# Layer 0's rows go back to node order through DRAM and indirect DMAs in a two-layer graph network kernel

## The chip, the cores and the metric

The kernel runs on one core of a Trainium2 chip. The metric is the time of one execution on the device, in microseconds. A core has a matrix engine (PE, with its weight loads listed apart as PEld), a vector engine (DVE), a scalar engine (ACT), GpSimd (POOL), and SyncE (SP), which here issues all DMAs. Each engine works through its own queue in order. TensorE's results go to PSUM, which PE writes and DVE and ACT read; POOL works on SBUF.

## The reference

There are 128 graphs of 128 nodes with 64 features, and a weighted adjacency matrix each. Layer 0 sums a two-layer edge function over the edges; layer 1 aggregates with the weights and applies a small network. Both have a residual and a layer norm. Cut to what is computed:

```
mask = adj > 0
h    = relu(x @ W1a [row j] + (x[j] - x[k]) @ W1b + b1)      # for every pair j, k
hm   = sum over k of h * mask
x    = layernorm(x + hm @ W2 + deg * b2)                     # layer 0
agg  = adj @ x
h    = elu(elu(agg @ V1 + c1) @ V2 + c2)
x    = layernorm(x + h @ V3 + c3)                            # layer 1
```

## The kernel before

Two graphs form a pair, and there are 64 pairs. The kernel uses that the masks are sparse. In a pair it counts each row's edges, ranks the rows by that count, and permutes them, so that rows with many edges stand together and are given many slots, and rows with few edges few. Edge sums are then dense matmuls with one-hot columns.

`prepare(p)` makes the mask `mk` on POOL (L419), the degrees on DVE, a key on POOL (`degb`, `keyc`, L427 and L428), and from it `pos`, for each row its place in sorted order (f32, 128 x 2, one column for each graph). `permb` (L450) is the permutation as a bf16 matrix. `sort_mask` (from L541) sorts the mask by two matmuls (L547), and by two more (L550) makes the inverse permutation. All four land in one PSUM bank; ACT copies the halves out as `mtp` (L555) and `permT` (L557, f32). `sort_x` and `project_a` sort and project the features; POOL splits the projections in bf16 parts `cp` (L493, L495) and computes `sa` and `corr`.

The units of the main loop are (pair, 3 feature groups, 3 banks): ACT seeds a PSUM bank `e` (L714), PE adds matmuls with the one-hot matrix (L725, L729), DVE reduces with absolute values into `sums` (L739).

`finish(p)` closes a pair. POOL subtracts the correction (`hm`, L642), PE projects to 64 outputs for each graph (L646 to L653), ACT copies the result to SBUF as `ys` (L657; 128 x 130, the two graphs' rows in sorted order and the degrees), and SP sends the degrees away (L659). `unsort` then brings the rows back to node order on PE: an identity matmul with `xx` puts the residual into the bank (L662) and a matmul with `permT` for each graph adds the rows (L664). `norm` copies the bank to `y` on ACT (L597), takes mean and variance on DVE (`st` L603, `ve` L605), the inverse root on POOL (`rs`, L610), the bias on DVE (`nb`, L613), and applies both on ACT (L619). The result `x1` is layer 0's output. Layer 1 follows: aggregation (L671), two hidden layers with `elu`, the last matmuls (L693 to L696), again `norm`, and the output DMA (L700). Each pair's loads (L406, L408) are issued three pairs ahead.

The order of the work is made by a planner, `Flow`, while the program is built. Every piece of work is a generator step that names its engine, an estimated cost, the events it needs and how many PSUM banks out of four. The planner always emits the step that can start first on its own clocks, with due times to break near ties. An event is the step's end by these clocks plus a lag of 0.2 us. A second name such as `PORT` makes steps on different engines exclude each other in the plan. Costs and events fix only the order in each queue; on the chip, semaphores make each instruction wait for its data. `ROUND` (13.0) is the planned length of a pair and `AHEAD` (3) how many pairs early preparation begins. A fallback for denser masks (`dense`) follows and isn't entered with this input.

Of the kernel before, what the change touches and what calls it, by code (L numbers as in the profile page):

```python
# [31 lines left out]
F32 = mybir.dt.float32  # L32
BF16 = mybir.dt.bfloat16
I32 = mybir.dt.int32
# [12 lines left out]
def gnn_kernel(ctx: ExitStack, tc: tile.TileContext, x, adj, w1, b1, w2, b2,  # L47
               v1, c1, v2, c2, v3, c3, out):
    nc = tc.nc
    B, N, F = x.shape  # L50
# [216 lines left out]
    with ExitStack() as fast:  # L267
        loads = fast.enter_context(tc.tile_pool(name="loads", bufs=8))
        prep = fast.enter_context(tc.tile_pool(name="prep", bufs=4))
        work = fast.enter_context(tc.tile_pool(name="work", bufs=4))  # L270
        ps_e = fast.enter_context(tc.tile_pool(name="ps_e", bufs=1, space=bass.MemoryType.PSUM))
        ps_m = fast.enter_context(tc.tile_pool(name="ps_m", bufs=1, space=bass.MemoryType.PSUM))
        sparse(tc, locals())
# [76 lines left out]
def sparse(tc, env):  # L350
# [5 lines left out]
    loads, prep, work, ps_m = g.loads, g.prep, g.work, g.ps_m  # L356
# [17 lines left out]
    PACE = ROUND / (3 * NB)  # L374
    STEP = 1.3
# [9 lines left out]
    def event(*key):  # L385
        return EV.setdefault(key, [])

    def happened(ev, *key):
        event(*key)[:] = ev
# [5 lines left out]
    def act(n, pointers=0):  # L395
        return 0.07 + 0.09 * pointers + n / 1200
# [4 lines left out]
    def pool(n):  # L401
        return 0.15 + n * 0.0022
# [7 lines left out]
    def flat(t):  # L410
        return t.rearrange("p s n -> p (s n)")

    def prepare(p):
# [38 lines left out]
        ev, = yield ("DVE PORT", 0.36, [ev], 0, permute)  # L452
# [88 lines left out]
    def sort_mask(p, ev):  # L541
# [3 lines left out]
        def sort(t):  # L545
            for s in range(2):
                nc.tensor.matmul(t[:, s * N:(s + 1) * N], d["mk"][:, s, :], permb[:, s, :],  # L547
                                 start=True, stop=True)
            for s in range(2):
                nc.tensor.matmul(t[:, (2 + s) * N:(3 + s) * N], permb[:, s, :], identb,  # L550
                                 start=True, stop=True)
        ev, t = yield ("PE", 0.33, [ev], 1, sort)
        mtp = d["mtp"] = prep.tile([P, 2, N], BF16, name="mtp", bufs=7)
        permT = d["permT"] = prep.tile([P, 2, N], F32, name="permT", bufs=7)
        evm, = yield ("ACT", act(2 * N), [ev], 0, lambda: nc.scalar.copy(flat(mtp), t[:, :2 * N]))  # L555
        happened(evm, "mtp", p)
        ev, = yield ("ACT", act(2 * N), [ev], 0, lambda: nc.scalar.copy(flat(permT), t[:, 2 * N:]))  # L557
        flow.give(t, ev)
        happened(ev, "permT", p)
# [34 lines left out]
    def norm(yps, ev, name):  # L594

        y = work.tile([P, 2, O], F32, name="y", bufs=6)
        evy, = yield ("ACT", act(2 * O), [ev], 0, lambda: nc.scalar.copy(flat(y), yps[:, :2 * O]))  # L597
# [3 lines left out]
        def stats():  # L601

            nc.vector.bn_stats(st.rearrange("p s t -> p (s t)"),  # L603
                               yps[:, :2 * F].rearrange("p (s f) -> p f s", s=2))
            nc.vector.tensor_scalar(ve, st[:, :, 2], 1.0 / F, EPS, op0=OP.mult, op1=OP.add)  # L605
        ev, = yield ("DVE", 0.38, [ev, evy], 0, stats)
        flow.give(yps, ev)
# [28 lines left out]
    def finish(p):  # L636
# [24 lines left out]
        def unsort(t):  # L661
            nc.tensor.matmul(t[:, :2 * O], ident, flat(xx), start=True, stop=False)  # L662
            for s in range(2):
                nc.tensor.matmul(t[:, s * O:(s + 1) * O], d["permT"][:, s, :],  # L664
                                 ys[:, s * O:(s + 1) * O], start=False, stop=(s == 1))
        ev, t = yield ("PE", 0.6, [ev, event("permT", p)], 1, unsort)
        x1, ev = yield from norm(t, ev, "x1")

# [30 lines left out]
        o, ev = yield from norm(t, ev, "o")  # L699
# [277 lines left out]
```

## Time and profile before

| | us |
|---|---|
| median of 3 runs | 928.74 |
| lowest and highest of them | 928.43, 929.03 |
| the profiled execution | 928.32 |
| its span in the trace | 925.7 |
| PE busy | 867.1 |
| DVE busy | 813.8 |
| ACT busy | 717.3 |
| POOL busy | 506.6 |

A profile comes from one execution. Its span runs from the first to the last instruction of the program, and 2.6 us lie around it. An engine's busy time is the time in which at least one of its instructions runs; shares are of the span or of a stretch of it. TensorE's granted clock was 0.991 of full speed in the mean. In the list of waits, a row names the engine and line that waited, what it waited for, the total us, how often, and the longest. In a tile's view the three numbers are shortest, median and longest duration in ns, then the first and the last start.

Three groups that the change touches look like this (busy us in all, mean ns of one):

| line and work | count | busy us | mean ns |
|---|---|---|---|
| L557, ACT copies `permT` | 64 | 24.3 | 380 |
| L597, ACT copies `y` (both layers) | 128 | 33.4 | 261 |
| L603, DVE statistics | 128 | 36.8 | 288 |

### The profile page before, as it was taken

Reading aid. Unit: us, or ns where it says so; the run is one execution under the profiler, and the core shown is the slowest. Engines: PE = TensorE matmul, PEld = TensorE weight load, DVE = VectorE, ACT = ScalarE, POOL = GpSimd, SP = SyncE. Lnnn points to the kernel's source line nnn. Section 1 sums busy time; section 2 is a strip of 40 time slices with the busy share of each in tenths; the row PEclk is TensorE's granted clock in tenths of the full one; section 3 lists DMA queues with packets and bytes.
Section 4 is the critical chain, followed back from the end, with each engine's and each line's share of the span. In section 5 each row is a group of like instructions: output and inputs, shape, how many; then the busy total and the mean of one; then the engine's idle time right before and its main releaser. Section 6 shows DMA issues by size and latency. Waiting matters only on the chain. (4 is left out here: it accounts for less than half of the span.)

```text
span 925.7 us, 19643 instructions
## 1 busy us (share of the span) xinstructions
PE 867.1 (94%) x6739; PEld 556.4 (60%) x6740; DVE 813.8 (88%) x2278; ACT 717.3 (77%) x2050; POOL 506.6 (55%) x654
## 2 busy tenths in 40 slices
PE   2689999999999999999999999999999999999994
PEld 1456666665665665666665666666666666666663
DVE  7699889989989989989989989999999999999972
ACT  0577887788788788788788788888878887888772
POOL 1565555665556565556565556565556555555521
PEclk9999999999999999999999999999999999999996
DMA  1100100100110110110100010110011001000000
GB/s 29 43 10 21 25 15 21 24 21 16 24 24 13 24 24 14 24 25 12 25 23 15 22 24 12 25 24 16 21 25 24 16 21 25 16 23 22 7 8 12
DMA packets 63580, 18.84 MB, mean 20 GB/s; under 512 B 46257, under 2 KB 63474, under 8 KB 63474
## 3 DMA queue, kind: packets, MB, share of 16 engines
q1 hardware_dynamic: 63474, 17.52, 8.1%
q8 instruction: 55, 0.90, 0.4%
q14 instruction: 51, 0.42, 0.1%
HBM read 13.24 MB, written 4.19 MB: 19 GB/s over the span
## 5 line engine op out<-in xcount | busy, mean ns | idle before, releaser
L739 DVE TENSOR_REDUCE sums<-e 128x56 f32<-128x504 f32 (+3 forms) x768 | 395.0, 542 | 33.6 <-PE e L725 16.9
L714 ACT COPY e<-aj 128x504 f32<-128x504 f32 (+2 forms) x768 | 366.1, 486 | 74.3 <-DVE sums L739 67.4
L725 PE MATMUL e<-oh,cp 128*128 128x504 bf16 (+1 forms) x1152 | 281.7, 375 | 1.8 <-ACT e L714 1.7
L610 POOL TENSOR_TENSOR rs<-ve,mhalf 128x2 f32<-128x2 f32 x128 | 90.6, 708 | 228.2 <-DVE ve L605 223.9
L725 PEld LDWEIGHTS <-cp 128*128 128x128 bf16 x1152 | 106.1, 97 | 89.5 <-DVE sums L739 1.1
L729 PE MATMUL e<-oh,cp 128*64 128x504 bf16 (+1 forms) x1152 | 157.5, 382 | 1.1 <-ACT e L714 1.1
L572 DVE TENSOR_TENSOR oh<-vp,slotc 128x1008 bf16<-128x1008 bf16 (+2 forms) x256 | 153.9, 601 | 3.2 <-ACT vp L564 3.0
L642 POOL TENSOR_TENSOR hm<-sums,corr 128x384 f32<-128x384 f32 x64 | 73.6, 1151 | 45.8 <-DVE sums L739 42.3
L629 ACT ACTIVATE e<-m,mone 128x256 f32<-128x256 f32 x128 | 62.6, 489 | 32.4 <-PE m L688 30.9
L493 POOL CAST cp<-r 128x512 bf16<-128x512 f32 x64 | 48.9, 765 | 70.5 <-DVE r L490 70.4
L729 PEld LDWEIGHTS <-cp 128*64 128x64 bf16 x1152 | 53.9, 109 | 42.9 <-issue 18.2
L495 POOL TENSOR_TENSOR cp<-r,cp 128x512 bf16<-128x512 f32 x64 | 74.5, 1164 | 5.0
L518 POOL TENSOR_TENSOR sa<-aj,srow 128x384 f32<-128x384 f32 x64 | 64.4, 1007 | 21.2 <-ACT aj L511 21.1
L538 POOL TENSOR_TENSOR corr<-ea,sa 128x384 f32<-128x384 f32 x64 | 67.2, 1050 | 3.6 <-DVE ea L532 2.6
L419 POOL TENSOR_SCALAR mk<-adj 128x256 bf16<-128x256 f32 x64 | 54.8, 856 | 21.3 <-DMA xx<-in_x_dram 20.9
L632 DVE SCALAR_TENSOR_TENSOR h<-e,m 128x256 f32<-128x256 f32 x128 | 52.5, 410 | 10.1 <-ACT e L629 9.3
L490 DVE TENSOR_TENSOR r<-m,cp 128x256 f32<-128x256 f32 x128 | 53.1, 416 | 6.5 <-ACT cp L486 6.1
L597 ACT COPY y<-m 128x128 f32<-128x128 f32 x128 | 33.4, 261 | 28.7 <-PE m L664 22.0
L619 ACT ACTIVATE o<-y,nb,rs 128x64 f32<-128x64 f32 x128 | 51.2, 467 | 3.0 <-DVE nb L613 3.0
L486 ACT CAST cp<-m 128x256 bf16<-128x256 f32 x128 | 49.5, 388 | 3.2 <-PE m L479 3.2
L619 ACT ACTIVATE x<-y,nb,rs 128x64 f32<-128x64 f32 x128 | 49.3, 433 | 3.3 <-DVE nb L613 1.6
L651 PE MATMUL m<-w2h,hm 128*128 128x64 f32 x256 | 48.1, 289 | 0.0
(189 smaller groups left out, 1731.5 us busy)
## 6 DMA issues: line engine op xcount, KB each, us to landing
adj<-in_adj_dram SPq DMA_DIRECT2D x64, 128.0 KB, 2.3
xx<-in_x_dram SPq DMA_DIRECT2D x64, 64.0 KB, 2.2
out_dram<-o SPq DMA_DIRECT2D x64, 64.0 KB, 1.7
degs<-ys SPq DMA_DIRECT2D x64, 1.0 KB, 1.7
w1a<-in_L_gnn_W_dram SPq DMA_DIRECT2D x2, 48.0 KB, 2.2
w1b<-in_L_gnn_W_dram SPq DMA_DIRECT2D x2, 48.0 KB, 2.1
v1d<-in_L_gnn_W_dram SPq DMA_DIRECT2D x2, 32.0 KB, 2.1
v2s<-in_L_gnn_W_dram SPq DMA_DIRECT2D x1, 64.0 KB, 2.0
```

Of the source, the lines that this page charges most:

```text
L495: lambda: nc.gpsimd.tensor_sub(cp[:, 2], r1, cp[:, 1]))
L518: evs, = yield ("POOL PORT", 1.0, [have], 0, lambda: nc.gpsimd.tensor_mul(sa, aj, g.srow))
L538: ev, = yield ("POOL PORT", 1.05, [ev, evs], 0, lambda: nc.gpsimd.tensor_sub(corr, ea, sa))
L572: lambda: nc.vector.tensor_tensor(oh[:, :, c].rearrange("p b (s w) -> p b s w", w=w), vp[:, :, p0:p1].rearrange("p b (o w) -> p b o w", o= ...
L610: lambda: nc.gpsimd.tensor_tensor(rs, ve, g.mhalf, op=OP.pow))
L619: nc.scalar.activation(o[:, s, :], y[:, s, :], AF.Identity, bias=nb[:, s:s + 1], scale=rs[:, s:s + 1])
L629: lambda: nc.scalar.activation(e, z, AF.Exp, bias=g.mone))
L642: lambda: nc.gpsimd.tensor_sub(hm, d["sums"], d["corr"]))
L714: nc.scalar.copy(e[:, off:off + sl * w].rearrange("p (s w) -> p s w", w=w), d["aj"][:, c:c + 1, p0:p1].to_broadcast([P, sl, w]))
L725: nc.tensor.matmul(e[:, :n], cp[:, k, c, 0:P], oh[:, c, base:base + n], start=False, stop=(k == 2), skip_group_check=True)
L729: nc.tensor.matmul(e[s * HB:(s + 1) * HB, :n], cp[:, k, s, P:H], oh[:, s, base:base + n], start=False, stop=(k == 2), skip_group_check=True)
L739: nc.vector.tensor_reduce(d["sums"][:, c, p0:p1], e[:, off:off + sl * w].rearrange("p (s w) -> p w s", w=w), AX.X, OP.add, apply_absolute_ ...
```

## The change

The inverse permutation matrix `permT` is no longer made, neither its matmuls nor its copy. `prepare` makes `posi`, the places as whole numbers, on POOL. In `finish`, SP writes the two graphs' sorted rows from `ys` to two scratch tensors in DRAM. POOL then issues an indirect DMA for each graph, which reads for every node the row at its place `posi`, into `y`. A POOL addition of `xx` gives `y1`. `norm` is handed an SBUF tile: layer 0 gives it `y1`, and layer 1 an ACT copy of its bank, which it made inside before. Statistics read that tile and no longer the bank. The planner is told 2.0 us on POOL for the two gathers, 0.45 for the addition, and `DMA` = 2.5 us for a transfer.

```diff
+        dram = fast.enter_context(tc.tile_pool(name="dram", bufs=8, space=bass.MemoryType.DRAM))
...
+    DMA = 2.5
...
-        ev, = yield ("DVE PORT", 0.36, [ev], 0, permute)
+        have = ev
+        ev, = yield ("DVE PORT", 0.36, [have], 0, permute)
+        posi = d["posi"] = prep.tile([P, 2], I32, name="posi", bufs=10)
+        e, = yield ("POOL PORT", pool(2), [have], 0,
+                    lambda: nc.gpsimd.tensor_copy(posi, pos))
+        happened(e, "posi", p)
...
-            for s in range(2):
-                nc.tensor.matmul(t[:, (2 + s) * N:(3 + s) * N], permb[:, s, :], identb,
-                                 start=True, stop=True)
-        ev, t = yield ("PE", 0.33, [ev], 1, sort)
+        ev, t = yield ("PE", 0.17, [ev], 1, sort)
...
-        permT = d["permT"] = prep.tile([P, 2, N], F32, name="permT", bufs=7)
         evm, = yield ("ACT", act(2 * N), [ev], 0, lambda: nc.scalar.copy(flat(mtp), t[:, :2 * N]))
+        flow.give(t, evm)
         happened(evm, "mtp", p)
-        ev, = yield ("ACT", act(2 * N), [ev], 0, lambda: nc.scalar.copy(flat(permT), t[:, 2 * N:]))
-        flow.give(t, ev)
-        happened(ev, "permT", p)
...
-    def norm(yps, ev, name):
-
-        y = work.tile([P, 2, O], F32, name="y", bufs=6)
-        evy, = yield ("ACT", act(2 * O), [ev], 0, lambda: nc.scalar.copy(flat(y), yps[:, :2 * O]))
+    def norm(y, ev, name):
+
...
             nc.vector.bn_stats(st.rearrange("p s t -> p (s t)"),
-                               yps[:, :2 * F].rearrange("p (s f) -> p f s", s=2))
+                               y.rearrange("p s f -> p f s"))
...
-        ev, = yield ("DVE", 0.38, [ev, evy], 0, stats)
-        flow.give(yps, ev)
+        ev, = yield ("DVE", 0.4, [ev], 0, stats)
...
-        def unsort(t):
-            nc.tensor.matmul(t[:, :2 * O], ident, flat(xx), start=True, stop=False)
-            for s in range(2):
-                nc.tensor.matmul(t[:, s * O:(s + 1) * O], d["permT"][:, s, :],
-                                 ys[:, s * O:(s + 1) * O], start=False, stop=(s == 1))
-        ev, t = yield ("PE", 0.6, [ev, event("permT", p)], 1, unsort)
-        x1, ev = yield from norm(t, ev, "x1")
+
+        rows = [dram.tile([N, O], F32, name=f"rows{s}") for s in range(2)]
+        for s in range(2):
+            nc.sync.dma_start(rows[s], ys[:, s * O:(s + 1) * O])
+        y = work.tile([P, 2, O], F32, name="y", bufs=8)
+
+        def unsort():
+            for s in range(2):
+                nc.gpsimd.indirect_dma_start(
+                    out=y[:, s, :], out_offset=None, in_=rows[s][:, :],
+                    in_offset=bass.IndirectOffsetOnAxis(ap=d["posi"][:, s:s + 1], axis=0))
+        ev, = yield ("POOL PORT", 2.0, [[ev[0] + DMA], event("posi", p)], 0, unsort)
+        y1 = work.tile([P, 2, O], F32, name="y1", bufs=8)
+        ev, = yield ("POOL PORT", 0.45, [[ev[0] + DMA]], 0,
+                     lambda: nc.gpsimd.tensor_add(y1, y, xx))
+        x1, ev = yield from norm(y1, ev, "x1")
...
-        o, ev = yield from norm(t, ev, "o")
+        y = work.tile([P, 2, O], F32, name="y2", bufs=6)
+        ev, = yield ("ACT", act(2 * O), [ev], 0, lambda: nc.scalar.copy(flat(y), t[:, :2 * O]))
+        flow.give(t, ev)
+        o, ev = yield from norm(y, ev, "o")
```

More of the change, by code (lines that the diff above doesn't have):

```diff
@@ L355, in sparse @@
     LAY, NB = g.LAY, g.NB
-    loads, prep, work, ps_m = g.loads, g.prep, g.work, g.ps_m
+    loads, prep, work, dram, ps_m = g.loads, g.prep, g.work, g.dram, g.ps_m
     ident, identb, onesf, onesb = g.ident, g.identb, g.onesf, g.onesb
```

## The prediction

> **What bounds the kernel now.** I read the head of the page first, then one long stretch of the steady part, then the waits, then single rounds in order of time. The stretch from 100 to 880 us shows how full each engine is once the start is over (busy us and instruction counts by engine, granted clock, DMA share):
>
> ```profile
> 100.00:880.00 780.00, 765.22 (x6015) 491.72 (x6016) 710.26 (x1951) 638.58 (x1831) 450.55 (x571) 1.00 0.09 20
> ```
>
> PE is busy 765.22 of 780 us (98.1%) at full clock, DVE 91.1%, ACT 81.9%, POOL 57.8%. So PE sets the pace, DVE is close behind it, and POOL is the engine with room. The list of waits says the same: POOL's largest waits are for DVE and none of any size is for PE to give something back.
>
> ```profile
> POOL rs L610 <- DVE ve L605: 223.9, 85, 8.7
> POOL cp L493 <- DVE r L490: 70.4, 43, 3.0
> POOL hm L642 <- DVE sums L739: 42.3, 62, 4.0
> ...
> PEld m L646 <- POOL hm L642: 4.6, 17, 0.6
> ```
>
> The last line is the one that matters later: PE does wait for POOL's `hm` in places, so there is little margin there. The unit of the rest is a round, one pair of graphs. The tile view of `ys` gives its length:
>
> ```profile
> L657 ACT COPY ys<-m x64: 258/262/268, 58.1 to 905.9; 128x130 f32<-128x130 f32 x64
> ```
>
> 905.9 - 58.1 = 847.8 us for 63 steps is 13.46 us a round. By the shares above, a round holds 13.20 us of PE, 12.26 of DVE, 11.02 of ACT and 7.78 of POOL.
>
> One round on PE, and the same place on POOL, in order of time (start, length, what):
>
> ```profile
> 511.02 0.39 PE L662 MATMUL m<-xx,ident 128*128 128x128 f32 x2
> 511.24 0.56 PE L664 MATMUL m<-ys,permT 128*128 128x64 f32 x4
> 511.63 0.27 PE L433 MATMUL m<-identb,degb 128*128 128x128 bf16 x2
> ...
> 514.17 0.71 POOL L610 TENSOR_TENSOR rs<-ve,mhalf 128x2 f32<-128x2 f32 x1 [1.50 <-DVE ve L605]
> 514.95 1.19 POOL L538 TENSOR_TENSOR corr<-ea,sa 128x384 f32<-128x384 f32 x1
> 518.75 0.70 POOL L610 TENSOR_TENSOR rs<-ve,mhalf 128x2 f32<-128x2 f32 x1 [2.61 <-DVE ve L605]
> ```
>
> The reader is to see that the unsort block really occupies PE (0.61 us from its first matmul to the next work), and that POOL has single holes of 2.6 and 1.5 us, not crumbs.
>
> **What the Trainium skill says.** "GPSIMD Engine Reference", section "When to use GPSIMD", has a DMA issued from that engine built by two of its own cores, which write the descriptors: an indirect DMA is POOL work, not only DMA work. No DMA of this kernel is issued by POOL, so the trace can't agree or disagree. "DMA: Bandwidth & Descriptors", section "Anatomy of one DMA — SWDGE (gpsimd) path", puts about 2.0 us on one such DMA end to end plus bytes at 436 GB/s, and its "Latency and other measured facts" some 1 us until the first byte. Nearest in this trace: SP's own DMAs land 1.7 us (64 KB out) and 2.2 us (64 KB in) after issue. "SBUF — State Buffer", section "Who interferes with whom", says that a DVE operation with two SBUF inputs, or in a two-port mode, and a POOL operation shut each other out. The trace agrees: `ve` (L605) takes 168 ns at least and 268 in the mean, `nb` (L613) 141 and 239, `permb` (L450) 238 and 272.
>
> **The change part by part.** *PE.* Gone are L550 (two bf16 matmuls that make `permT`), L662 (residual) and L664 (the inverse permutation). I take each matmul's start to the start of the next one in PE's order between 100 and 880 us: L664 25.1 us, L662 14.2, L550 8.0, in all 47.3 of 780, that is 0.82 us a round. PE's need falls from 13.20 to 12.38. *ACT.* Gone are the `permT` copy (L557, 380 ns) and, of the two `y` copies at L597, the layer-0 one (261 ns): 0.64 us. ACT at 11.0 us bounds nothing, so I cost this at nothing; PE and DVE cover it. *PSUM.* The bank of the mask sort comes back one copy earlier, the unsort bank isn't taken at all, and the second norm's bank is free after the copy. Between nothing and 0.1 us a round of gain; I take nothing, since PE's 1.9% of idle time holds few bank waits.
>
> *SP.* Two writes of 32 KB follow the `degs` DMA, at 471 ns of issue each by the `degs` row. Behind them stand the loads of the pair three rounds ahead and later outputs; SP sits waiting most of the round, so 0.94 us costs nothing. It does set when the rows exist: 0.03 us from `ys` to the first issue, two issues of 0.47, and 1.7 to land make 2.67 us after `ys`. The planner counts on 2.7 (lag 0.2 and `DMA` 2.5), so a wait at this point should be short.
>
> *POOL.* The index copy `posi` has two elements: 0.20 us like `keyc` (L428, 203 ns) to 0.41 like `degb` (L427, 413); I take 0.4. The residual add has 128 elements: `keyc` gives the fixed 0.19 and `sa` (384 elements, 1.00 us) the slope, so 0.46. The two gathers are the unknown. The planner's own 2.0 for the pair is no measurement. From below I take 0.67 each, a 256-element POOL pass (L419, 0.86 us) less the fixed 0.19 of `keyc`: an estimate, for 128 reads and 128 writes to be written out. From above, 2.1 each, the page's whole end-to-end time held on the engine. I take 1.2, a little above the page's time to the first byte, for the index has to be read too. Sum: 0.4 + 2.4 + 0.46 = 3.3 us; POOL goes from 7.78 to 11.0 of 13.1, or 84%. This fits, since the gathers have the 2.6 us hole behind `corr` (the rows written at about 511.9 land near 514.6) and the add the next one. Queued behind a gather that waits for its rows are `rs`, `mk`, `hm`, `cp`; DVE waits for `rs`, PE for `hm`.
>
> *DVE.* Its work stays: the statistics read SBUF instead of PSUM (288 ns; plus or minus 0.06, I take nothing). More POOL time means more mutual exclusion. `ve` and `nb` now lose (0.10 + 0.10) x 2 = 0.4 us a round beside 7.78 us of POOL; 42% more POOL adds 0.17. Nothing if the gathers only write, 0.5 if they lock DVE out for their whole length; I take 0.2, and DVE needs 12.46.
>
> *The sum.* With PE at 12.38 and DVE at 12.46 neither has cover from the other any more: what is late next is DVE, which now shows gaps before most of its instructions. PE reaches 98% when alone at the bound; I let DVE reach 95% when two engines are. 12.46 / 0.95 = 13.11 us, 0.35 less than now, and over 63 rounds -22 us.
>
> *The end.* The last pair has no work beside it. Today `ys` (905.88 + 0.27) leads to the statistics 1.45 us later:
>
> ```profile
> 905.88 0.27 ACT L657 COPY ys<-m 128x130 f32<-128x130 f32 x1 [0.45 <-PE m L653]
> ...
> 907.60 0.30 DVE L603 BATCH_NORM_STATS2 st<-m 128x6 f32<-128x128 f32 x1 [0.17 <-ACT y L597]
> ```
>
> Then it takes 2.67 + 0.1 + 1.2 (first gather) + 2.1 (second, to its landing) + 0.1 + 0.46 + 0.1 = 6.73 us: +5.3. The profiled execution took 928.3 us (span 925.7 and 2.6 around it): 928.3 - 22 + 5.3 = 911.6. It lies 0.4 below the median of the runs, so I say 912.
>
> **Rivals.** *A, slower: POOL's queue stops PE.* Place: the gather pair stands in front of `hm` and `rs` in POOL's fixed order. The plan reserves 2.0 us. If a gather takes I and its landing is d later than planned, what is behind is late by 2I - 2.0 + d; the margin at L646 is about 0.5 us (the waits on `hm` reach 0.6), and the rest stops PE. With PE at 12.38 plus its usual 0.25 of idle, I = 1.6 and d = 0.4 give a stop of 1.1 and a round of 13.74: 63 x 0.28 + 5.3 = +23, about 952. It decides from a round of 13.38 on (5.3 / 63 below now), a stop of 0.75, which is I of about 1.4. For it: no row prices the gather, and the queue is in order. Against it: the holes are as long as the pair. *B, hidden: DVE is the bound.* If the exclusion costs 0.4 instead of 0.2, or DVE keeps its 92% share of the round, the round is 13.3 to 13.5 and the time 924 to 936; I say 931. For it: DVE's 91%. Against it: many of DVE's waits are for PE (`sums` L739 waits 29 us for L725 and L729). *C, all of it:* PE stays the bound at 98.1%, 12.38 / 0.981 = 12.62 a round: -53 + 5.3, about 881. Against it: DVE would have to be 98.7% busy. That the change doesn't do what it says I leave out: the matmuls and copies are plainly gone from the diff.
>
> **How the numbers follow.** Forecast 0.40 (its own range 899 to 925), A 0.36, B 0.16, C 0.08. The range for 8 in 10 leaves out most of C and the upper third of A: 897 to 956, which also takes in I from 0.9 to 1.6. No change is within 0.2%, some 1.9 us, which is about what a measurement of this kernel can tell. Of B I put 0.03 on faster, 0.06 on the same and 0.07 on slower. Faster: 0.40 + 0.08 + 0.03 = 0.51; same 0.06; slower 0.36 + 0.07 = 0.43.
>
> **What would show it.** Right: starts of `ys` 13.1 us apart, PE near 95% and DVE near 95% busy, gathers about 1.2 us apart on POOL, the add reading its rows within 3 us of the second gather. A shows as PE waiting at L646 or the x1 matmuls for POOL, with POOL waiting on row writes or gathers for tens of us in total; B as DVE above 95% with `ve`, `nb` and `permb` longer. I am wrong if gathers take over 1.4 us of POOL each, or if the time from `ys` to the statistics grows by much more than 5.3 us.

## The result, and the profile after

The changed kernel takes 955.17 us (median, 954.12 to 956.70) beside 928.59 for the kernel before on the same chip: a ratio of 1.0288, with a 95% interval of 1.027 to 1.0306. It is slower by 26.6 us, where 912 was forecast. The profiled execution has a span of 952.3 us, against 925.7.

The head of the page, of the kernel after (busy us and share of the span, instructions), and its chain of waits by engine and by line:

```profile
span 952.3 us, 18831 instructions
...
PE 877.5 (92%) x6227; PEld 508.3 (53%) x6228; DVE 861.7 (90%) x2278; ACT 702.9 (74%) x1922; POOL 680.4 (71%) x910
...
DVE 49%; PE 22%; issue 10%; ACT 10%; DMA 4%; POOL 4%; SPq 1%; ACTq 0%; DVEq 0%; POOLq 0%
DVE sums L749 18%; DVE oh L573 9%; DVE nb L611 4%; PE e L739 4%; PE e L735 4%; ACT e L724 3%; DVE cmp L443 3%; DVE r L497 3%; DVE st L602 2%; DVE h L630 2%; DVE ve L604 2%; DVE permb L452 2%; PE m L695 2%; DMA y<-rows,posi 2%; PE m L511 1%
```

DVE's busy time grew by 47.9 us although no DVE work was added, and half of the chain that ended last runs on DVE. (The page of the kernel before has no such chain to set beside it; that of a kernel with the order of before follows below.) PE is busy for 10 us longer than before, with fewer matmuls. The stretch from 100 to 880 us of the kernel after (PE, PEld, DVE, ACT, POOL, then clock, DMA share, GB/s):

```profile
100.00:880.00 780.00, 756.28 (x5447) 438.17 (x5445) 738.74 (x1911) 616.37 (x1690) 596.13 (x790) 1.00 0.13 30
```

DVE went from 91.1% of this stretch to 94.7%, POOL from 57.8% to 76.4%. Where DVE's time went is in the groups by shape, of the kernel after (count | busy us, mean ns | idle before, releaser):

```profile
L611 DVE SCALAR_TENSOR_TENSOR nb<-st,rs 128x2 f32<-128x2 f32 x128 | 59.6, 466 | 9.5 <-POOL rs L608 9.3
L573 DVE TENSOR_TENSOR oh<-vp,slotc 128x660 bf16<-128x660 bf16 x64 | 52.3, 818 | 0.1
L452 DVE TENSOR_SCALAR permb<-iotb,pos 128x128 bf16<-128x128 bf16 x128 | 44.7, 390 | 0.0
L573 DVE TENSOR_TENSOR oh<-vp,slotc 128x352 bf16<-128x352 bf16 x64 | 30.7, 480 | 0.2
```

In the kernel before these four took 239, 525, 272 and 337 ns in the mean; the first two, before:

```profile
L613 DVE SCALAR_TENSOR_TENSOR nb<-st,rs 128x2 f32<-128x2 f32 x128 | 30.6, 239 | 9.7 <-POOL rs L610 8.1
L572 DVE TENSOR_TENSOR oh<-vp,slotc 128x660 bf16<-128x660 bf16 x64 | 33.6, 525 | 0.1
```

The same instructions on the same data now last 1.4 to 2 times as long: `nb` writes two numbers per partition and takes 466 ns. Not all got longer: the 1008-wide `oh` went from 771 to 728 ns. The groups on POOL that the change brought, and the waits that rival A was about, after:

```profile
L667 POOL DMA_INDIRECT y<-rows,posi x128 | 132.1, 1032 | 63.5 <-DMA rows<-ys 40.7 <-issue 22.8
L673 POOL TENSOR_TENSOR y<-y,xx 128x128 f32<-128x128 f32 x64 | 34.9, 546 | 12.5 <-DMA y<-rows,posi 11.9 <-issue 0.7
L458 POOL CAST posi<-pos 128x2 int32<-128x2 f32 x64 | 12.1, 190 | 30.8 <-DVE cmp L443 30.7
```

```profile
POOL rs L608 <- DVE ve L604: 45.3, 83, 8.7
POOL y L667 <- DMA rows<-ys: 40.7, 47, 4.7
PEld m L678 <- ACT x L617: 33.0, 59, 3.3
...
PEld m L644 <- POOL hm L640: 2.3, 9, 0.5
```

A gather costs 1.03 us, less than the forecast's 1.2. POOL does wait 40.7 us for row writes, but PE's wait for `hm` at L644 (L646 before) is 2.3 us in all, half of what it was. POOL's wait for DVE at `rs` fell from 223.9 to 45.3 us: most of POOL's holes are gone. PE instead waits 33.0 us for `x1`, which needs `nb` (9.6 us before). That wait isn't made by `nb`'s length alone: it is still 27 to 29 us in kernels below where `nb` is short or made on POOL.

Split by the starts of `ys`, the span's 26.6 us are: first `ys` at 60.6 instead of 58.1 (+2.5), 63 rounds of 13.710 instead of 13.457 us (+15.9), and 28.0 us from the last `ys` to the end instead of 19.8 (+8.2).

What holds DVE up can be seen in order of time. One norm, and further on one `oh`, of the kernel after (start, length, what):

```profile
505.76 1.08 POOL L608 TENSOR_TENSOR rs<-ve,mhalf 128x2 f32<-128x2 f32 x1 [0.33 <-DVE ve L604]
...
506.82 0.99 POOL L640 TENSOR_TENSOR hm<-sums,corr 128x384 f32<-128x384 f32 x1
...
507.10 0.73 DVE L611 SCALAR_TENSOR_TENSOR nb<-st,rs 128x2 f32<-128x2 f32 x1
...
507.86 0.77 ACT L617 ACTIVATE x<-y,nb,rs 128x64 f32<-128x64 f32 x2 [0.28 <-DVE nb L611]
...
510.34 1.16 POOL L502 TENSOR_TENSOR cp<-r,cp 128x512 bf16<-128x512 f32 x1
...
510.76 1.10 DVE L573 TENSOR_TENSOR oh<-vp,slotc 128x660 bf16<-128x660 bf16 x1
```

`rs` is followed at once by `hm` on POOL. `nb` starts 0.28 us later and ends at 507.83, when `hm` does (507.81): it takes 0.73 us instead of the 0.14 that it needs. The 660-wide `oh` (482 ns at its shortest) starts under `cp`, lasts 1.10 us and ends 0.36 us behind it. "SBUF — State Buffer", section "Who interferes with whom", of the Trainium skill states the rule: a DVE instruction with two SBUF inputs contends with a GpSimd instruction that reads SBUF, and the port pair that they share is an exclusive lock. The trace agrees for `nb` behind `hm`, in length and in where the ends fall.

Two norms of the kernel before, for comparison:

```profile
403.18 0.71 POOL L610 TENSOR_TENSOR rs<-ve,mhalf 128x2 f32<-128x2 f32 x1 [1.49 <-DVE ve L605]
...
403.96 1.20 POOL L538 TENSOR_TENSOR corr<-ea,sa 128x384 f32<-128x384 f32 x1
...
405.73 0.14 DVE L613 SCALAR_TENSOR_TENSOR nb<-st,rs 128x2 f32<-128x2 f32 x1
...
408.43 0.86 POOL L419 TENSOR_SCALAR mk<-adj 128x256 bf16<-128x256 f32 x1
408.50 0.35 DVE L613 SCALAR_TENSOR_TENSOR nb<-st,rs 128x2 f32<-128x2 f32 x1 [0.16 <-POOL rs L610]
```

There too an operation that reads stands right behind the root, `corr`; but in DVE's queue other work stands before `nb`, which starts 1.8 us after the root and meets nothing. Counted over the 128 norms by the POOL operation beside `nb`, before: 68 meet none (146 ns in the mean), 59 meet `mk` (348). After: 47 meet `hm` (735), 37 the new addition (408), 20 `mk` (314). So both queues' orders matter, and one of the two new neighbours is work of the change itself. (Without that addition, in an experiment below, `nb` meets `mk` 59 times and `hm` 47 times and stays at 444 ns.) Beside `mk`, which reads SBUF as well, `nb` ends 0.45 us before `mk` does (59 of these), so the trace doesn't show every reading POOL operation holding it to its end. `oh` likewise: 34 of the 256 start under the `cp` of the example and take 1.10 us in the mean; before, 2 did.

### The profile page after: what moved, and what is told of

Same layout as the page of the kernel before. It is cut to its first block, busy times and chain, and to the rows that moved or that the text cites. A ratio compares the mean times of both kernels' runs of the same rounds, so it can differ in the third digit from the quotient of the medians.

```text
span 952.3 us, 18831 instructions
## 1 busy us (share of the span) xinstructions
PE 877.5 (92%) x6227; PEld 508.3 (53%) x6228; DVE 861.7 (90%) x2278; ACT 702.9 (74%) x1922; POOL 680.4 (71%) x910
## 4 chain that ended last, share of the span: by engine, by line
DVE 49%; PE 22%; issue 10%; ACT 10%; DMA 4%; POOL 4%; SPq 1%; ACTq 0%; DVEq 0%; POOLq 0%
DVE sums L749 18%; DVE oh L573 9%; DVE nb L611 4%; PE e L739 4%; PE e L735 4%; ACT e L724 3%; DVE cmp L443 3%; DVE r L497 3%; DVE st L602 2%; DVE h L630 2%; DVE ve L604 2%; DVE permb L452 2%; PE m L695 2%; DMA y<-rows,posi 2%; PE m L511 1%
## 5 line engine op out<-in xcount | busy, mean ns | idle before, releaser
L749 DVE TENSOR_REDUCE sums<-e 128x56 f32<-128x504 f32 (+3 forms) x768 | 388.8, 540 | 8.4 <-PE e L735 6.1
L573 DVE TENSOR_TENSOR oh<-vp,slotc 128x1008 bf16<-128x1008 bf16 (+2 forms) x256 | 176.2, 688 | 2.8 <-ACT vp L565 1.8
L667 POOL DMA_INDIRECT y<-rows,posi x128 | 132.1, 1032 | 63.5 <-DMA rows<-ys 40.7
L608 POOL TENSOR_TENSOR rs<-ve,mhalf 128x2 f32<-128x2 f32 x128 | 100.6, 787 | 48.6 <-DVE ve L604 45.3
L500 POOL CAST cp<-r 128x512 bf16<-128x512 f32 x64 | 44.0, 688 | 45.5 <-DVE r L497 45.5
L640 POOL TENSOR_TENSOR hm<-sums,corr 128x384 f32<-128x384 f32 x64 | 68.2, 1066 | 9.8 <-DVE sums L749 9.0
L421 POOL TENSOR_SCALAR mk<-adj 128x256 bf16<-128x256 f32 x64 | 60.1, 939 | 21.1 <-DMA xx<-in_x_dram 20.8
L611 DVE SCALAR_TENSOR_TENSOR nb<-st,rs 128x2 f32<-128x2 f32 x128 | 59.6, 466 | 9.5 <-POOL rs L608 9.3
L617 ACT ACTIVATE x<-y,nb,rs 128x64 f32<-128x64 f32 x128 | 49.5, 435 | 17.8 <-DVE nb L611 17.4
L467 ACT CAST permf<-permb 128x256 f32<-128x256 bf16 x64 | 25.8, 404 | 49.5 <-DVE permb L452 49.5
L602 DVE BATCH_NORM_STATS2 st<-y 128x6 f32<-128x128 f32 x128 | 37.1, 290 | 24.4 <-ACT y L707 19.8
```

The costliest lines, as they stand in the source:

```text
L573: lambda: nc.vector.tensor_tensor(oh[:, :, c].rearrange("p b (s w) -> p b s w", w=w), vp[:, :, p0:p1].rearrange("p b (o w) -> p b o w", o= ...
L608: lambda: nc.gpsimd.tensor_tensor(rs, ve, g.mhalf, op=OP.pow))
L611: lambda: nc.vector.scalar_tensor_tensor(nb, st[:, :, 1], -1.0, rs, op0=OP.mult, op1=OP.mult))
L617: nc.scalar.activation(o[:, s, :], y[:, s, :], AF.Identity, bias=nb[:, s:s + 1], scale=rs[:, s:s + 1])
L640: lambda: nc.gpsimd.tensor_sub(hm, d["sums"], d["corr"]))
L667: nc.gpsimd.indirect_dma_start(out=y[:, s, :], out_offset=None, in_=rows[s][:, :], in_offset=bass.IndirectOffsetOnAxis(ap=d["posi"][:, s:s ...
```

## The experiments

For each kernel I worked out a *round* (from the 4th start of `ys` to the 6th last, 55 rounds), the busy us of PE, DVE and POOL in it, and DVE's *shut-out time*: for `oh`, `nb`, `permb` and `ve`, each duration less the shortest of its shape in any of these kernels, summed per round, whatever lengthened it. Each ratio is to the kernel before on the same chip, where its median lay between 928.1 and 929.0 us. "Old order" kernels keep the instruction order of the kernel before, "new order" that of the kernel after; "replanned" lets the planner choose.

| kernel | order | time us | ratio to before, 95% | round | PE | DVE | POOL | shut-out | `nb` ns |
|---|---|---|---|---|---|---|---|---|---|
| before | old | 928.6 |  | 13.60 | 13.34 | 12.38 | 7.88 | 0.72 | 239 |
| after | new | 955.2 | 1.0288 [1.0270, 1.0306] | 13.88 | 13.46 | 13.15 | 10.59 | 1.80 | 466 |
| no gathers | new | 931.7 | 1.0026 [1.0017, 1.0036] | 13.56 | 13.30 | 12.87 | 8.54 | 1.50 | 457 |
| no addition | new | 959.8 | 1.0334 [1.0317, 1.0351] | 14.01 | 13.47 | 13.36 | 10.11 | 2.04 | 444 |
| `nb` on POOL | new | 932.6 | 1.0049 [1.0032, 1.0067] | 13.44 | 13.04 | 12.20 | 11.10 | 0.87 |  |
| all POOL work dead | old | 933.3 | 1.0050 [1.0035, 1.0066] | 13.67 | 13.37 | 12.51 | 10.75 | 0.99 | 252 |
| before, `nb` on POOL | old | 933.2 | 1.0042 [1.0025, 1.0059] | 13.68 | 13.36 | 12.18 | 8.28 | 0.56 |  |
| before, no permutation | old | 907.4 | 0.9771 [0.9755, 0.9788] | 13.23 | 12.92 | 12.24 | 7.88 | 0.73 | 239 |
| rows first | new | 951.2 | 1.0229 [1.0206, 1.0253] | 13.81 | 13.43 | 13.11 | 10.63 | 1.73 | 476 |
| short memset | new | 958.8 | 1.0323 [1.0305, 1.0340] | 13.92 | 13.45 | 13.12 | 10.86 | 1.74 | 391 |
| long memset | new | 939.5 | 1.0133 [1.0116, 1.0150] | 13.58 | 13.16 | 12.41 | 11.41 | 1.19 | 176 |
| copy that reads | new | 950.0 | 1.0233 [1.0216, 1.0250] | 13.74 | 13.31 | 12.71 | 11.79 | 1.45 | 411 |
| dead matmuls | new | 971.1 | 1.0454 [1.0437, 1.0472] | 14.16 | 13.87 | 13.14 | 10.60 | 1.71 | 420 |
| accumulating gathers | new | 968.7 | 1.0418 [1.0400, 1.0435] | 14.07 | 13.16 | 13.08 | 11.94 | 1.72 |  |
| `nb` and rows | replanned | 977.3 | 1.0520 [1.0502, 1.0537] | 14.19 | 13.33 | 13.04 | 10.90 | 1.58 |  |
| `DMA` 3.2 | replanned | 955.9 | 1.0287 [1.0270, 1.0304] | 13.85 | 13.24 | 12.99 | 10.41 | 1.59 | 295 |
| `ROUND` 12.6 | replanned | 996.0 | 1.0731 [1.0716, 1.0747] | 14.76 | 13.56 | 13.38 | 10.43 | 2.08 | 315 |
| `nb` and rows | new | 925.5 | 0.9970 [0.9961, 0.9979] | 13.37 | 13.04 | 12.03 | 11.17 | 0.64 |  |

### Is it POOL's load?

The whole of the new POOL and DMA work was put into the kernel before, with its order, its permutation matmuls and its results kept; nobody reads what the gathers bring.

```diff
+        posi = d["posi"] = prep.tile([P, 2], I32, name="posi", bufs=10)
+        nc.gpsimd.tensor_copy(posi, pos)
...
+        for s in range(2):
+            nc.sync.dma_start(rows[s], ys[:, s * O:(s + 1) * O])
...
+        for s in range(2):
+            nc.gpsimd.indirect_dma_start(
+                out=yd[:, s, :], out_offset=None, in_=rows[s][:, :],
+                in_offset=bass.IndirectOffsetOnAxis(ap=d["posi"][:, s:s + 1], axis=0))
...
+        nc.gpsimd.tensor_add(yd1, yd, xx)
```

> The kernel before with its plan and its PE unsort kept, and the new POOL and DMA work put beside it for nothing: the index copy, the row writes, the two gathers and an addition, whose result nobody reads. X: POOL rises to about 10.7 us a round and DVE's blocked time by 0.4 to 1 us: 945 to 970. W: POOL holds up cp and hm where it waits: 935 to 960, with waits of PE for POOL. L: no chain is longer, so no change: 928 to 932.

933.3 us, 4.5 more than its own kernel before. Two groups of this kernel, and its chain by engine:

```profile
L676 POOL DMA_INDIRECT yd<-rows,posi x128 | 141.0, 1101 | 30.5 <-issue 29.8 <-DMA rows<-ys 0.7
L616 DVE SCALAR_TENSOR_TENSOR nb<-st,rs 128x2 f32<-128x2 f32 x128 | 32.2, 252 | 18.7 <-POOL rs L613 18.5
```

```profile
PE 59%; DVE 19%; ACT 15%; issue 3%; POOL 2%; DMA 1%; SPq 1%; DVEq 0%; ACTq 0%; POOLq 0%
```

POOL is as busy as in the kernel after (10.75 us a round), the gathers cost as much, and `nb` stays at 252 ns. The load alone isn't the loss. Two limits: nothing waits for these gathers, and the new work has harmless neighbours where I put it. 63 of the `nb` run beside a gather and take 151 ns, 58 meet `mk` as before, and none meets the dead addition.

### The gathers or the addition left out

In the first of two kernels the row writes and the gathers are left out, so layer 0's rows stay in sorted order (the addition reads `ys`); in the second the addition is left out, so the residual is missing. Both keep the new order.

```diff
-        for s in range(2):
-            nc.sync.dma_start(rows[s], ys[:, s * O:(s + 1) * O])
...
-            for s in range(2):
-                nc.gpsimd.indirect_dma_start(
...
+            pass
...
-                     lambda: nc.gpsimd.tensor_add(y1, y, xx))
+                     lambda: nc.gpsimd.tensor_add(
+                         y1, ys[:, :2 * O].rearrange("p (s f) -> p s f", s=2), xx))
```

> The changed kernel with its plan (every queue's order) kept, but without the row writes and the gathers: the addition reads the sorted rows in SBUF, so the return to node order is left out. Three theories. X (exclusion): DVE is the bound, because its operations with two SBUF inputs or in a two-port mode now meet POOL operations back to back. The gathers themselves block DVE for only about 0.1 us a round, but 2.1 us of POOL time and 0.9 us of its waits go, so POOL stands earlier and meets other DVE operations: 925 to 940, with nb and oh still longer than before the change. W (POOL's queue): what costs is POOL held by the gathers and by their waits on DMAs: 915 or less. L (length of the chain through DRAM): about 8 us of the end go and the steady part gains too: 930 to 945.

```diff
-                     lambda: nc.gpsimd.tensor_add(y1, y, xx))
-        x1, ev = yield from norm(y1, ev, "x1")
+                     lambda: None)
+        x1, ev = yield from norm(y, ev, "x1")
```

> The changed kernel with its plan kept, but without the residual addition on POOL (layer 0's residual is left out; norm reads the gathered rows). POOL has 0.56 us a round less. X: the 0.16 us of nb that the addition blocks and some of the rest go: 942 to 950. W: POOL's queue is 0.7 us shorter, with its wait for the gather moved to DVE: 940 to 955. L: 0.6 us off each chain, nothing in the steady part: 953 to 955.

Without gathers it is 931.7 us, 23.5 back. Even with the transfers and 2.05 us of POOL a round gone, and with the permutation matmuls gone too, the new order only just reaches the kernel before; `nb` stays at 457 ns. Without the addition it is 959.8, slower than the change itself with less to do. That was a miss: nothing I had priced explains a loss from leaving work out. POOL's wait for row writes rose there from 40.7 to 66.6 us and the shut-out time to 2.04, which points again to what stands beside what; it isn't shown that these two make the loss.

In the first of them the end gives a second reading. From the last `ys` to the end it still takes 27.6 us, with no DMA between `ys` and the statistics. Its last statistics, in order of time:

```profile
911.00 0.29 DVE L602 BATCH_NORM_STATS2 st<-y 128x6 f32<-128x128 f32 x1 [1.50 <-ACT y L703]
...
911.40 0.29 DVE L602 BATCH_NORM_STATS2 st<-y 128x6 f32<-128x128 f32 x1
```

The last pair's statistics (911.40) stand in DVE's queue behind the output statistics of the pair before (911.00), which wait for that pair's layer 1. So the new order puts a second chain of the same length there.

### `nb` taken off DVE

The bias is made on POOL right behind the root, from a negated mean that DVE writes beside `ve`. No instruction changes its place otherwise.

```diff
+            nc.vector.tensor_scalar(nm, st[:, :, 1], -1.0, None, op0=OP.mult)
...
+        def root():
+            nc.gpsimd.tensor_tensor(rs, ve, g.mhalf, op=OP.pow)
+            nc.gpsimd.tensor_mul(nb, nm, rs)
...
-                     lambda: nc.vector.scalar_tensor_tensor(nb, st[:, :, 1], -1.0, rs,
-                                                            op0=OP.mult, op1=OP.mult))
+                     lambda: None)
```

> The changed kernel with its plan kept, but nb (minus mean times inverse root) is no longer a DVE operation with two SBUF inputs: DVE writes minus the mean beside ve, and POOL multiplies right behind the root. DVE loses 0.98 us of nb a round and gains about 0.35; POOL gains 0.4. X: DVE is the bound, so the round falls by 0.4 to 0.6 us: 918 to 932. W: POOL's queue is longer by 0.4 us a round: 955 to 975. L: no change, 950 to 958.

The same edit in the kernel before:

> The kernel before with its plan kept, and nb moved from DVE to POOL as in e3. There POOL has holes behind the root, and nb costs DVE only 0.48 us a round, against 0.35 for the new operation beside ve. X (exclusion, which the change made worse): hardly anything to win, 924 to 931. If moving nb wins as much here as in the changed kernel (22 us), it is a gain of its own and no sign of what the change did: 905 to 912.

In the kernel after it brings back 22.5 us, all of it in the rounds; in the kernel before it costs 4. The chain of the first, by engine:

```profile
PE 56%; DVE 23%; ACT 9%; issue 6%; POOL 3%; DMA 2%; SPq 1%; POOLq 0%; DVEq 0%; ACTq 0%
```

DVE falls from 49% of the chain to 23%, although POOL works half a microsecond a round more. So the place of `nb` is a cost of the new order, not of the kernel.

### `nb` left on DVE, and POOL kept out of its way

A move might have helped only because DVE had less to do. So `nb` stays, and behind each root POOL first writes zeros to a tile of its own, which reads nothing: 128 columns, then 512. The control puts a copy of 448 columns there, which reads.

```diff
+        gap = work.tile([P, 4 * P], F32, name="gap", bufs=2)
+
+        def root():
+            nc.gpsimd.tensor_tensor(rs, ve, g.mhalf, op=OP.pow)
+            nc.gpsimd.memset(gap, 0.0)
```

> The changed kernel with its plan kept, and on POOL, right behind each inverse root, a memset of a tile that nobody reads (about 0.2 us each, 0.4 us of POOL a round). It writes SBUF and reads nothing, and it holds back hm, which reads two SBUF inputs, just long enough for nb to start on DVE. X (exclusion: nb stands behind hm): nb falls from 466 ns to 200 or less and 12 to 25 us come back, though POOL has more to do: 930 to 943. W (POOL's queue is what costs): slower, 958 to 980. Neither, if the loss lies elsewhere in the order: 950 to 960.

> The changed kernel in its own order, with a POOL memset of 128x512 (about 0.5 us, writes only, no input) behind each inverse root, so that the bias on DVE can get in before the next POOL operation with inputs. POOL's load grows by about 1 us a round. Theory X (the bias is shut out by the operation that follows the root, and that lengthens the chain of the norm and DVE's work): nb falls from 466 to under 250 ns in the mean and the time to 930-948. Rival (moving nb in the earlier run gained only because DVE had one operation less): nb falls but the time is 955 or more, since POOL has more to do. If nb doesn't fall, the test is open.

> The control to the long shield (939.5 us, nb 176 ns): the same kernel and the same place, but the POOL operation behind each root now reads SBUF too (a copy of 128x448 from a constant tile, about 0.5 us) where the memset only wrote. If nb is shut out by a POOL operation that reads, it waits for this copy now: nb 450-700 ns in the mean, and the time 955-980, no better than the change itself. If the long shield gained for another reason (a later start of what follows the root, that is timing alone), nb stays under 250 ns and the time at 935-945.

The short one, 196 ns, mostly ended before `nb` reached DVE (some 0.26 us after the root): 391 ns in the mean, and 958.8 us. That time lies where the theory of POOL's queue had put it; but since only 43 of the 128 `nb` run beside the memset (159 ns) and 39 still meet `hm` (759), it doesn't test the other. With the long one POOL has 0.8 us a round more to do and the kernel is 15.6 us faster than the change, at 939.5. Its groups, its chain by engine, and one norm in order of time:

```profile
L611 POOL MEMSET gap<- 128x512 f32 x128 | 66.1, 516 | 0.0
...
L616 DVE SCALAR_TENSOR_TENSOR nb<-st,rs 128x2 f32<-128x2 f32 x128 | 22.5, 176 | 15.9 <-POOL rs L610 15.1
```

```profile
PE 52%; DVE 22%; ACT 10%; POOL 6%; issue 6%; DMA 2%; SPq 1%; ACTq 0%; DVEq 0%; POOLq 0%
```

```profile
506.68 0.82 POOL L610 TENSOR_TENSOR rs<-ve,mhalf 128x2 f32<-128x2 f32 x1
...
507.45 0.52 POOL L611 MEMSET gap<- 128x512 f32 x1
...
507.75 0.15 DVE L616 SCALAR_TENSOR_TENSOR nb<-st,rs 128x2 f32<-128x2 f32 x1
...
507.94 0.99 POOL L645 TENSOR_TENSOR hm<-sums,corr 128x384 f32<-128x384 f32 x1
```

`nb` runs beside the memset in 0.15 us. In the control, the same place:

```profile
509.06 0.82 POOL L613 COPY gap<-quiet 128x448 f32<-128x448 f32 x1
...
509.38 0.51 DVE L618 SCALAR_TENSOR_TENSOR nb<-st,rs 128x2 f32<-128x2 f32 x1
```

It ends with the copy again, and its mean is 411 ns. This is the skill's second half of the rule, that a POOL operation which only writes doesn't contend with such an instruction, and both kernels agree with it. The control's `nb` and time, 950.0 us, lie between what the two theories expected: 10.5 us of the memset's gain go when the filler reads, and 5 stay. The 10.5 are not all due to the reading: the copy is also longer, 633 ns in the mean against 516, and POOL has 0.38 us a round more to do. The 5 come with a shorter `oh` (601 ns against 688 in the kernel after), which suggests that a mere shift of POOL's later work changes who meets whom as well.

### PE's share in the bound

In the kernel before, the two matmuls that make the inverse permutation, its copy and the matmuls that apply it are left out; the residual matmul stays. Layer 0's rows are then neither unsorted nor added.

```diff
-                nc.tensor.matmul(t[:, (2 + s) * N:(3 + s) * N], permb[:, s, :], identb,
-                                 start=True, stop=True)
...
-            nc.tensor.matmul(t[:, :2 * O], ident, flat(xx), start=True, stop=False)
-            for s in range(2):
-                nc.tensor.matmul(t[:, s * O:(s + 1) * O], d["permT"][:, s, :],
-                                 ys[:, s * O:(s + 1) * O], start=False, stop=(s == 1))
+            nc.tensor.matmul(t[:, :2 * O], ident, flat(xx), start=True, stop=True)
```

> The kernel before with its plan kept; of the unsort on PE only the residual's matmul is left, and permT is neither made nor copied (layer 0's neighbour term is left out). By start-to-start times PE loses 0.57 us a round and ACT 0.38; nothing is added on POOL, DVE or the DMA queues. P (PE sets the pace, as the prediction had it): the round falls by all of it: 890 to 896. Q (a part of PE's time is already spent waiting, and DVE and the order around it set the pace): 912 to 924.

And the reverse in the kernel after, three dead matmuls behind each pair's adjacency transposes:

```diff
+            nc.tensor.matmul(t[:, 256:384], ident, flat(XX[p]), start=True, stop=False)
+            for s in range(2):
+                nc.tensor.matmul(t[:, 256 + s * O:256 + (s + 1) * O], ident, XX[p][:, s, :],
+                                 start=False, stop=(s == 1))
```

> The changed kernel with its plan kept, and matmuls for nothing on PE (one f32 128 x 128 and two f32 128 x 64, as the removed unsort had), put behind the transposes of adj, where nothing waits for them soon: about 0.6 us of PE a round. P (PE still sets the pace in the changed kernel): 975 to 995. X (DVE and its blocked operations set it): 955 to 965.

By the working of the prediction, 25.1 + 8.0 us of 780, or 0.57 us a round, were taken away in the first, 36 us in 63 rounds. The rounds became 0.352 us shorter, 22.2 us: 62%, with ACT's copy of `permT` gone as well. In the second, by the same measure, some 0.70 us a round, 44 us, were added, and the rounds became 0.293 us longer, 18.5 us: 42%. PE is part of the bound in both kernels and all of it in neither. The Trainium skill, "Perfetto Trace Analysis", section "Identifying the Most-Contended Engine", says that matmul busy time is not a good measure of how close PE is to its limit, since matmuls are pipelined; these two kernels agree that it isn't one. For DVE the section takes the share of busy time as a fair measure. Here it is not quite that: DVE's 13.15 busy us a round in the kernel after hold instructions that last 1.80 us longer in all than they need.

### POOL's waits for transfers

Rows before degrees on SP (the `degs` DMA moved behind the row writes); the planner told 3.2 us for a transfer; and gathers that add onto `xx`, with no POOL addition (on top of rows first and `nb` on POOL):

```diff
-    DMA = 2.5
+    DMA = 3.2
...
-                    out=y[:, s, :], out_offset=None, in_=rows[s][:, :],
-                    in_offset=bass.IndirectOffsetOnAxis(ap=d["posi"][:, s:s + 1], axis=0))
+                    out=xx[:, s, :], out_offset=None, in_=rows[s][:, :],
+                    in_offset=bass.IndirectOffsetOnAxis(ap=d["posi"][:, s:s + 1], axis=0),
+                    compute_op=OP.add)
```

> The changed kernel with its plan kept; SP issues the two row writes ahead of the degrees' DMA, so the rows land about 0.5 us earlier. W (POOL's waits on row writes, 40.7 us in 47 waits, hold up hm, rs and cp): 20 us or more come back, 925 to 938. X: POOL's waits shrink, but DVE's blocked operations stay: 945 to 955.

> The changed kernel with one number of the plan changed: DMA is 3.2 us, not 2.5, so that POOL's queue reaches the gathers and the addition later, when rows and gathers have really landed. The work is the same; only the order in the queues differs. W: POOL's waits on DMAs (52 us) go and with them 15 us or more: 925 to 940. X: the waits go, but which POOL operation stands beside which DVE operation falls anew; anything from 930 to 980, and the time then follows DVE's blocked time and not POOL's waits.

> The changed kernel with its plan kept, e3's nb on POOL and e7's row writes, and the residual added by the gathers themselves (they accumulate onto the features in SBUF), so that POOL's addition goes. Against e3 (932.6) POOL loses 0.56 us a round and the chain 0.6 us, if the accumulating gather costs POOL and the DMA engines no more than the plain one. X: 915 to 932. W: 910 to 925. If the accumulating gathers are slower by more than 0.5 us each: 935 or more.

Rows first cuts the row wait from 40.7 to 15.2 us and gains 4.0 us. The longer planned transfer cuts it to 17.8 and the time doesn't move (955.9). So these waits are a small part of the loss. The second also says that shut-out time isn't the whole: it fell to 1.59 us a round and `nb` to 295 ns, with no gain. The accumulating gather is dearer; the kernel takes 968.7 us, against 925.5 with the plain one:

```profile
L671 POOL DMA_INDIRECT xx<-rows,posi x128 | 209.0, 1633 | 63.9 <-PE m L699 18.0 <-issue 10.9 <-DMA rows<-ys 9.7
```

1.63 us of POOL each instead of 1.03, and it lands 3.2 us after issue instead of 2.5. Two of them cost 1.2 us more than two plain ones, and the addition that they spare takes 0.55.

### The order alone, and the two gains together

The changed kernel with the planned round 12.6 instead of 13.0 has the same instructions in another order. The other two have `nb` on POOL and rows first, once replanned (the root step told as 0.92 us) and once in the new order.

> The changed kernel, its instructions the same, with the planned length of a round 12.6 us instead of 13.0; only the order changes. If the loss sits in which operations stand beside each other (order), the time moves by more than 5 us one way or the other, with the blocked time of DVE (now 2.1 us a round) moving along with it. If the loss is the load of POOL and the number of instructions, it stays at 953-958 and DVE's blocked time at 2.0-2.2.

> The changed kernel with e3's nb and e7's row writes, and the plan told of it (root and nb 0.92 us on POOL in one step, no DVE step). X: at least e3's gain, 915 to 932. W: 940 or more with the longer POOL queue.

> The changed kernel in its own order with two edits together: the bias nb made on POOL right behind the root from a negated mean that DVE writes beside ve (932.6 us alone), and the rows written to DRAM before the degrees (951.2 alone against 955.2). If the two are independent: 932.6 - 4 = 928 to 930, no different from the kernel before. If POOL's waits for the rows are covered once nb is gone: 932-934.

996.0 us for the first: the order, with all that follows from it, is worth 41 us. Its shut-out time rose from 1.80 to 2.08 (the expectation gave 2.1 for the kernel after, which isn't the table's count). In the replanned one the same work as in the last costs 977.3 instead of 925.5, a difference of 52. In the first, `permb` shows what an order does:

```profile
L452 DVE TENSOR_SCALAR permb<-iotb,pos 128x128 bf16<-128x128 bf16 x128 | 62.7, 576 | 0.0
```

It takes 576 ns against 390 in the kernel after and 272 before. ACT waits 40.9 us for it, but 49.5 in the kernel after, so this wait doesn't make the difference. Nor does shut-out time explain all of that kernel: its round is 1.38 us above DVE's busy time (0.73 in the kernel after), its POOL waits 100.8 us for rows, and its granted clock in the steady stretch is 0.97. I didn't trace the rest of the loss of the two replanned kernels to one mechanism.

The last kernel, the change with both edits in the new order, is 0.3% faster than the kernel before, a little better than expected, and the fastest here that computes everything. Its chain, by engine:

```profile
PE 70%; DVE 14%; ACT 7%; issue 4%; POOL 2%; SPq 1%; DMA 1%; POOLq 0%; DVEq 0%; ACTq 0%
```

## Why the prediction was wrong

*The step that failed* is DVE's part of the sum: "42% more POOL adds 0.17 ... I take 0.2, and DVE needs 12.46". DVE's shut-out time rose not by 0.2 but by 1.08 us a round, from 0.72 to 1.80: `oh` by 0.43, `nb` by 0.49, `permb` by 0.18, `ve` by nothing. Its busy time rose by 0.77, to 13.15 (records that overlap count once there; the sum of their lengths rose by 1.04). The divisor held: DVE is busy 94.7% of the steady stretch, and 13.15 / 0.95 is 13.84, near the round of 13.88. I had scaled the old exclusion by POOL's busy time and looked at `ve` and `nb` only; `oh`, DVE's second-largest group, has two SBUF inputs too. And of the skill's rule the prediction left out that beside two SBUF inputs only a POOL operation that reads SBUF counts. The scaling is what the dead load refutes: 36% more POOL work in the old order adds 0.27 us of shut-out time and 4.5 us to the kernel. What counts is which POOL operation runs when which DVE operation starts. The planner ordered the queues anew and filled POOL's holes, and `hm` or the new addition came to stand right behind `rs`, where `nb` follows.

*How much of the loss this is.* Adding what was measured in the old order, 13.457 + 0.066 (dead load) - 0.352 (no permutation), gives 13.17 us a round, an estimate that takes the two as independent, near the forecast's 13.11. The real round is 13.71. So 0.54 us a round, 34 us, came with the new order and with what the dead load leaves out: a norm that waits for its rows through DRAM. The kernel without gathers has no such path, and its round, 13.367, is 0.26 above the old order without permutation (13.105), which lacks the addition. So about half of the 0.54 is there before any transfer. Taking `nb` off DVE returns 0.373, with rows first 0.438, more than the 0.253 by which the change lengthened the rounds; the end stays at 27.6 and 27.9 us. The rest isn't assigned.

*PE.* The removed 0.82 us a round were read rightly from the trace, but not as PE's need: its busy time rose from 13.34 to 13.46 us a round while the matmuls became fewer (its share of the steady stretch fell only from 98.1% to 97.0%). Some of the matmuls that stay have longer records, those of `v2s` 413 ns against 380; why is not shown. "PE sets the pace" was 62% true by the measured saving. For the forecast this mattered less than DVE.

*POOL and SP.* Gathers 1.03 us (1.2 forecast), index copy 0.19 (0.4), addition 0.55 (0.46): POOL grew by 2.7 us a round, not by 3.3. "POOL goes to 84%" became 76%. SP's issues cost about what was said (0.43 us in the median, 0.53 in the mean, against 0.47). Nothing more was seen of ACT's and PSUM's part.

*The end* was forecast at +5.3 and cost 8.2 us. The last steps of the kernel after:

```profile
924.32 0.27 ACT L655 COPY ys<-m 128x130 f32<-128x130 f32 x1 [0.71 <-PE m L651]
924.62 0.47 SPq L657 DMA_DIRECT2D degs<-ys  x1
...
925.44 0.80 SPq L662 DMA_DIRECT2D rows<-ys  x2
...
927.94 1.02 POOL L667 DMA_INDIRECT y<-rows,posi  x1 [2.56 <-DMA rows<-ys]
...
929.26 0.96 POOL L667 DMA_INDIRECT y<-rows,posi  x1 [0.30 <-issue]
...
931.87 0.45 POOL L673 TENSOR_TENSOR y<-y,xx 128x128 f32<-128x128 f32 x1 [1.65 <-DMA y<-rows,posi]
932.07 0.27 ACT L707 COPY y<-m 128x128 f32<-128x128 f32 x1 [1.66 <-PE m L703]
932.37 0.30 DVE L602 BATCH_NORM_STATS2 st<-y 128x6 f32<-128x128 f32 x1 [1.50 <-ACT y L707]
...
932.77 0.29 DVE L602 BATCH_NORM_STATS2 st<-y 128x6 f32<-128x128 f32 x1
```

From the end of `ys` to the statistics it is 8.2 us, 6.7 more than before and not 5.3: the gather starts 3.35 us after `ys`, not 2.67. The sum had left out that `degs` is issued ahead of the rows: 0.47 us, and 0.35 more until the first row write. The chain that I summed is there, but beside it, and as long, is the pair before's output norm (932.37). The kernel without gathers ends hardly sooner (27.6 us after the last `ys` against 28.0), so shortening the DMA path alone would have given little. The 2.5 us at the start were not in the sum at all.

*The rivals.* A had the size, 952, and the wrong mechanism: gathers stayed under 1.4 us and PE hardly waited for POOL's `hm`. B had the mechanism, exclusion that makes DVE the bound, with `nb` and `permb` longer as its sign, but priced it at 0.4 us a round where 1.08 was measured, and so came out at 931 instead of 955. Of its signs, `nb` and `permb` got longer, `ve` did not (264 ns against 268), and DVE reached 94.7%, not over 95; and the dead matmuls show PE still a part of the bound.

## What to carry to other kernels

Exclusion between DVE and POOL is a matter of neighbours, not of load: ask of each DVE instruction with two SBUF inputs which POOL operation will be running when it starts, above all where a short one hangs on a POOL result, and give that POOL operation a successor that doesn't read, let the short one start later in DVE's queue, or make its result on POOL as well. When a change makes a planner order the queues anew, its cost is the load plus a new order, and the order can be worth more (41 us here, by one number of the plan); put the load in dead with the old order, and leave parts of the change out with the new order kept, to tell them apart. A busy share of PE near 98% isn't a bound until taking matmuls out has shown it.

## What the runs showed of the hardware

- A two-element DVE operation can be held for nearly a whole POOL instruction: `nb` ranges from 147 to 962 ns in the kernel after. With a POOL memset of 0.52 us behind each root it takes 176 ns in the mean, with a POOL copy of 0.63 us 411. Beside `mk` it takes 348 ns and ends 0.45 us before `mk`; beside a gather it takes 151 (dead load).
- An indirect gather of 128 rows of 256 bytes holds POOL for 0.94 us at least and 1.03 in the mean, and lands 2.5 us after issue (2.3 to 3.9), for which "DMA: Bandwidth & Descriptors" of the Trainium skill (section "Anatomy of one DMA — SWDGE (gpsimd) path") has about 2.0 plus the bytes. While running, gathers shut DVE out for under 0.1 us a round in the kernel after, and 0.15 with the dead load.
- An accumulating gather holds POOL for 1.63 us and lands after 3.2.
